# Another order for the end of a linear attention and for the routing behind it, in a two-layer vision tower

## The chip, the cores and the metric

The kernel runs as one program on one core of one Trainium2 chip. The metric is the device time of one execution in microseconds (us); where several runs are given, their median. All arithmetic is in 32-bit floating point.

A core has a matrix engine (TensorE, PE in the profile, with its weight loads as PEld), a vector engine (VectorE, DVE), an engine for activation functions (ScalarE, ACT), a general one (GpSimd, POOL), and SyncE (SP), which only issues transfers here. Each engine works through its own queue of instructions in order; an instruction that waits holds up all behind it on that engine, and nothing on the others unless they need its result.

## The reference

128 images go through a tokenizer, then two layers; each layer adds an attention and a feed-forward part to its input. What the change touches is the second layer: a linear attention over 8 heads, and the routing of 8192 tokens to 8 experts.

```python
# second layer, attention: q, k, v per head, x is normalised
q = softmax(q, axis=-1)
k = softmax(k, axis=-2)
q = q * sqrt(d)
attn_weights = einsum('bhnd,bhmd->bhnm', q, k).sum(0)       # not returned
context = einsum('bhnd,bhne->bhde', k, v)
out = einsum('bhnd,bhde->hbne', q, context)
# second layer, mixture of experts: T = 8192 tokens, E = 8, capacity C = 1280
logits = x @ gate_w + gate_b                                # x is normalised
probs = softmax(logits, axis=-1)
idx = argmax(probs, axis=-1)
prb = take_along_axis(probs, idx[:, None], axis=1)[:, 0]
one_hot = jax.nn.one_hot(idx, E)
pos = (cumsum(one_hot, axis=0) * one_hot).sum(-1) - 1       # place in the expert's buffer
kept = pos < C
hmid = relu(buf @ w1 + b1); ybuf = hmid @ w2 + b2           # per expert
y_tok = ybuf[idx, min(pos, C - 1)] * (prb * kept)[:, None]
return h + y_tok
```

## The kernel before

The program has stages one behind the other: tokenizer, an attention with relu, an attention of experts, then `linear_attention` (L1388), `route` (L1934) and `experts` (L2049). The data of the layer, h, is 128 images x 64 tokens x 256 features.

**The linear attention** takes the heads in four groups of two (`heads[0]` to `heads[3]`, class `Heads`). For each group a loop runs over 16 steps i. In a step TensorE projects queries and keys (`queries_keys`), `prepare` normalises and transposes token groups for later steps, then come the pieces of work that a table (`at(n, i, ...)`, in loop n at step i, in the order in which they were entered) puts there, and at last VectorE takes the projection out of PSUM (`queries_keys_kept`, L1478). The order of instructions on each engine is that of the program text (`manual_schedule`). The softmax, scores, mixing and sums of a group are put into the loop of the next one. For the last group, `heads[3]`, half of this is in the table and the rest in a function of its own, `last()` (L1740), which runs once behind the loops.

For one group the pieces are, with the engine that does most of each:

- `largest_of`, `maximum_of`, `spread_of`: the largest query over all (VectorE; TensorE for `pm`, L1533, and `pb`, L1542), `q_less_of` subtracts it (VectorE), `q_exp_of` (ScalarE);
- `k_max` (VectorE, L1580), `k_less` (GpSimd, L1584), `k_exp_of` (ScalarE), `k_sum` (VectorE, L1591), `k_over_sum` (GpSimd, one half of the last group VectorE, L1597);
- `values` (TensorE L1488, ScalarE copies), `values_transposed` (TensorE L1501, ScalarE L1504);
- `scores` (128 matmuls, L1606), `scores_kept` and `scores_sums` (`am`, `rq`, VectorE), then four times `mixed` (TensorE, L1628) and `added` (VectorE adds the mix to h, L1636);
- `written`: SyncE stores the group's 64 features of h to `hx` and to `out`, 2 MB each (L1640);
- `moments`: one `bn_stats` for each token (VectorE, L1644, written to `sth`), which the routing's normalisation needs;
- `transposed`: h transposed (TensorE L1650, ScalarE copies L1654), `gates`: its product with the gate's weights into a PSUM tile `pg` (L1663), `gates_added`: VectorE sums this over the four groups in `lgs` (L1673 and L1675).

Before, group 0 has its 64 moments in the loop, group 1 has 16 in the loop at step 8 and 48 in `last()`, groups 2 and 3 have all in `last()`. `routing.statistics` (L1903) then makes mean and variance of each token out of the moments, and ends with the inverse root (`inverse_root`, L1921, 14 small VectorE instructions).

**The routing** transposes the summed gates (`pl`, L1960), normalises them (`dev`, L1961, `pb`), finds each token's expert (`oh`), its place by a scan (`cs`, L1980) and two matmuls over partitions (`pp`), and the experts of the 39 blocks of 256 places (`past`, `be`, `bexp`, L2000 to L2004). Then it builds a table that says which token stands at each place: eight parts of 8 token columns each, with one-hot rows `lh` (L2029) and `hv` (L2032) by VectorE in rings of two buffers, `hv` times the token's number by ScalarE (64 activations in all, L2037), and 64 matmuls into `pi` (L2039). The table itself is `rin` and `rout` (L2042, L2046). Here no order is written out: the framework's planner orders each engine's instructions.

**The experts**, 39 blocks, load their weights (SyncE, L2097 to L2101) by the block's expert in `bexp`, and gather their tokens with indirect transfers by `rin` (GpSimd, L2110). The first three blocks' loads are issued ahead of the loop.

`c.busy` issues matmuls whose result nobody reads.

Of the kernel before, what the change touches and what calls it, by code (L numbers as in the profile page):

```python
# [12 lines left out]
F32 = mybir.dt.float32  # L13
# [7 lines left out]
P = 128  # L21
B = 128
# [1365 lines left out]
def linear_attention(c, front, hd, hx, out, k):  # L1388
# [8 lines left out]
    with (  # L1397
# [51 lines left out]
        class Heads:  # L1449


            def __init__(self, n, groups):
                self.n, self.groups = n, groups

            def begin(self):
                self.qk = hp.tile([P, 2, 32, P], F32, tag="qk", name="qk", bufs=2)
# [201 lines left out]

            def gates(self, x):

                self.pg = pso.tile([P, 4, B], F32, tag="po", name="pg")
                for s in range(4):
                    nc.tensor.matmul(  # L1663
                        self.pg[s * 32 : s * 32 + 32].rearrange("p j b -> p (j b)"),
                        wgs[:, self.n, :],
                        self.hT[s].rearrange("p j b -> p (j b)"),
                        start=True,
                        stop=True,
                    )

            def gates_added(self, x):
                if self.n == 0:
                    nc.vector.tensor_copy(lgs[:, x], self.pg)  # L1673
                else:
                    nc.vector.tensor_add(lgs[:, x], lgs[:, x], self.pg)  # L1675
# [9 lines left out]
        for n, x in enumerate(heads[:3]):  # L1685
# [30 lines left out]

            for k in range(8):
                at(m + 1, 1 + k, x.transposed, k)
            for k in range(4 if n == 0 else 1):
                at(m + 1, 8 + k, x.moments, 16 * k, 16)  # L1720
            for k in range(2):
                at(m + 1, 4 + 4 * k, x.gates, k)
                at(m + 1, 5 + 4 * k, x.gates_added, k)
# [15 lines left out]

        def last():  # L1740

            x, y, z = heads[3], heads[2], heads[1]
            x.values(0)
            x.largest_of(1)
            x.values(1)
            x.values(2)
            x.maximum_of(1)
            x.k_max(1)
            x.k_less(1, 0)
            x.k_less(1, 1)  # L1750
            x.values(3)
            x.spread_of(1)
            x.q_less_of(1, 0)
            x.values(4)
            x.q_exp_of(1, 0)
            x.q_less_of(1, 1)
            x.values(5)
            x.k_exp_of(1, 0)
            x.q_exp_of(1, 1)
            x.values(6)  # L1760
            x.k_exp_of(1, 1)
            x.values(7)
            x.k_sum(1)
            x.k_over_sum(1, 1)
            x.k_over_sum(1, 0)
            z.moments(16, 32)
            for i in range(2):
                x.values_transposed(i)
            x.scores()
            x.scores_kept()  # L1770
            x.values_transposed(2)
            x.scores_sums()
            x.values_transposed(3)
# [10 lines left out]
            for i in range(4):  # L1784
                y.transposed(i)
            y.gates(0)
            x.moments(0, 64)
            for i in range(4, 8):
                y.transposed(i)
            y.gates_added(0)  # L1790
            y.gates(1)
            y.moments(48, 16)
            for i in range(4):
                x.transposed(i)
            y.gates_added(1)
            routing.statistics(front.group(0), front.group(1))
            x.gates(0)
            x.gates_added(0)
            for i in range(4, 8):
                x.transposed(i)  # L1800
            x.gates(1)
            x.gates_added(1)

        def prepare(g, i):

# [46 lines left out]
class Routing:  # L1852
# [50 lines left out]
    def statistics(self, t, u):  # L1903

        nc, mean = self.c.nc, self.mean
        dev, sq = (t[:, 2 * i : 2 * i + 2].rearrange("p a (t n) -> p (a t) n", n=8) for i in range(2))
        var, m = (u[:, i, 0:T] for i in range(2))
        parts = self.sth.rearrange("p t n (s k) -> p t (n s) k", k=3)
        nc.vector.tensor_reduce(mean, parts[:, :, :, 1], AX.X, ALU.add)
        nc.vector.tensor_scalar_mul(mean, mean, 1.0 / 8)  # L1910
        nc.vector.tensor_sub(dev, parts[:, :, :, 1], bcast(mean, 2, 8))
        nc.vector.tensor_mul(sq, dev, dev)
        nc.vector.tensor_reduce(m, sq, AX.X, ALU.add)
        nc.vector.tensor_reduce(var, parts[:, :, :, 2], AX.X, ALU.add)
# [19 lines left out]
def route(c, k, gfd):  # L1934
# [4 lines left out]
    tc, nc = c.tc, c.nc  # L1939
    with (  # L1940
        tc.tile_pool(name="mg", bufs=1) as gp,
        tc.tile_pool(name="mn", bufs=2) as np_,
        tc.tile_pool(name="mgp", bufs=1, space=PSUM) as gpp,
    ):

        def g8(name):
# [11 lines left out]
        for x in range(2):  # L1958
            for j in range(4):
                nc.tensor.transpose(pl[:, x, j].rearrange("p s n -> p (s n)"), k.lgs[:, x, j, :], c.ident)  # L1960
        nc.vector.tensor_mul(dev, bcast(k.wsum, 1, T), bcast(mean, 2, E))  # L1961
        for x in range(2):
            ts = slice(x * 32, x * 32 + 32)
            o, i = (y[:, ts, :].rearrange("p (s j n) e -> p j s (n e)", s=4, j=4) for y in (pb, dev))
            for j in range(4):
                nc.vector.tensor_sub(o[:, j], pl[:, x, j, :, 0 : 2 * E], i[:, j])
# [14 lines left out]
        pp = gpp.tile([P, 2, E], F32, name="pp")  # L1981
        nc.tensor.matmul(pp[:, 0], k.before, cs[:, T - 1, :], start=True, stop=True)
        nc.tensor.matmul(pp[:, 1], k.ones, cs[:, T - 1, :], start=True, stop=True)
# [13 lines left out]
        nc.vector.tensor_sub(first, end, nblk)  # L1997
        nc.vector.tensor_scalar_mul(first, first, float(BLK))

        nc.vector.tensor_tensor(past, bcast(k.blk, 2, E), bcast(end, 1, NBLK), ALU.is_ge)  # L2000
        nc.vector.tensor_reduce(be[:, 0:NBLK], past, AX.X, ALU.add)
        nc.vector.tensor_scalar_min(be[:, 0:NBLK], be[:, 0:NBLK], float(E - 1))
        nc.vector.tensor_copy(be[:, NBLK : NBLK + 1], end[:, E - 1 : E])
        nc.vector.tensor_copy(c.bexp, be)  # L2004
# [15 lines left out]
        nc.vector.tensor_single_scalar(row[:, 1], row[:, 0], 7, ALU.arith_shift_right)  # L2020
        nc.vector.tensor_single_scalar(row[:, 2], row[:, 0], P - 1, ALU.bitwise_and)
        nc.vector.tensor_copy(at, row[:, 1:3])
        pi = gpp.tile([P, NTILE], F32, name="pi")
        NQ = 8
        for t0 in range(0, T, T // NQ):
# [9 lines left out]
            for i in range(T // NQ):  # L2035
                t = slice(t0 + i, t0 + i + 1)
                nc.scalar.activation(hv[:, i], hv[:, i], AF.Copy, scale=k.token[:, t])  # L2037
            for i in range(T // NQ):
                nc.tensor.matmul(pi, lh[:, i], hv[:, i], start=(t0 + i == 0), stop=(t0 + i == T - 1))  # L2039
        id1 = gp.tile([P, NTILE], F32, name="id1")  # L2040
# [286 lines left out]
```

## Time and profile before

| | us |
|---|---|
| median of 3 runs | 2665.02 |
| the runs | 2665.02, 2655.38, 2665.51 |
| the profiled execution | 2654.66 |
| its span, first to last instruction | 2652.9 |
| loop of the last head group ends (last L1478) | 2124.51 to 2125.20 |
| scores of the last group (L1606) | 2143.48 to 2148.93 |
| last sums into h (L1636) end, stores issued (L1640) | 2163.42, 2163.45 |
| `dev`, first VectorE instruction of the routing (L1961) | 2184.67 |
| first part of the table (L2029) | 2201.17 |
| first load of expert weights issued (L2097) | 2200.78 |
| table complete in PSUM, `rin` (L2042) | 2221.87 |
| first matmul of an expert (L2153) | 2231.16 |

Times inside an execution count from its first instruction. The stages named in the table fill about 110 of the 2653 us; behind them the experts run to the end. In a line of the timeline there stand the start and the length in us, the engine, the line of the program, the instruction with its output and inputs and how many of them were merged, and in brackets how long the engine was idle before it and what ended that.

### The profile page before, as it was taken

The numbers are of one execution on the slowest core, as the hardware profiler recorded it, in microseconds if no ns is written. First come the engines' busy times: TensorE is split into PE (matmuls) and PEld (weight loads), VectorE is DVE, ScalarE is ACT, GpSimd is POOL, SyncE is SP. The second block draws the span as 40 slices with busy tenths as digits, with TensorE's granted clock in tenths as the row PEclk, the third lists the DMA queues.
The fourth block names the chain that finished last, engine by engine and source line by source line (L and its number), as shares of the span: only waits on it lengthen the run. The fifth ranks groups of instructions, "written<-read, shape, count | busy, mean of one in ns | idle before, by whom it ended". The sixth has DMA issues, their size and how long they took to land. (4 is left out here: it accounts for less than half of the span.)

```text
span 2652.9 us, 81755 instructions
## 1 busy us (share of the span) xinstructions
PE 2526.2 (95%) x35633; PEld 1730.8 (65%) x35633; DVE 2012.2 (76%) x3000; ACT 1623.1 (61%) x3421; POOL 1625.8 (61%) x1428
## 2 busy tenths in 40 slices
PE   8989999999999999899999999999999877999997
PEld 4554444444444444688888888888566556888886
DVE  5759999999999999887878777878467786444443
ACT  2218889899898888666666666666344533233232
POOL 3319989899899999566565666653233313544544
PEclk9999999999999999999999999999999998999998
DMA  3100000000000000000000000000334444555554
GB/s 112 33 13 1 2 2 2 1 2 2 2 2 1 2 13 2 3 28 23 14 23 14 13 24 13 14 23 23 75 73 111 96 128 152 191 185 202 188 189 134
DMA packets 138046, 141.19 MB, mean 53 GB/s; under 512 B 108001, under 2 KB 121859, under 8 KB 129870
## 3 DMA queue, kind: packets, MB, share of 16 engines
q1 hardware_dynamic: 128684, 119.48, 15.3%
q0 software_dynamic: 7648, 14.77, 1.8%
q8 instruction: 281, 4.60, 0.7%
q10 hardware_dynamic: 1344, 1.61, 0.2%
q14 instruction: 89, 0.73, 0.1%
HBM read 104.00 MB, written 32.54 MB: 51 GB/s over the span
## 5 line engine op out<-in xcount | busy, mean ns | idle before, releaser
L540 POOL TENSOR_TENSOR m<-q,k 128x1024 f32<-128x1024 f32 x384 | 719.6, 1907 | 55.9 <-PE sc L342 46.8
L532 DVE TENSOR_TENSOR m<-pc,k 128x2048 f32<-128x2048 f32 (+1 forms) x320 | 646.3, 2055 | 0.5 <-ACT q L472 0.5
L342 PE MATMUL sc<-m,wide 128*32 128x512 f32 x4096 | 520.0, 597 | 8.9 <-ACT m L541 6.6
L541 ACT ACTIVATE m<-m 128x1024 f32<-128x1024 f32 x384 | 402.5, 1049 | 20.4 <-POOL m L540 20.4
L342 PEld LDWEIGHTS sc<-m,wide 128*32 128x32 f32 x4096 | 134.7, 109 | 269.2 <-issue 157.4
L550 ACT ACTIVATE m<-k,q 128x64 f32<-128x64 f32 x1024 | 270.8, 339 | 0.9 <-DVE k L419 0.9
L1070 DVE TENSOR_REDUCE mx<-sc 128x16 f32<-128x1024 f32 x128 | 156.0, 1219 | 133.6 <-PE sc L1058 133.6
L1085 POOL TENSOR_TENSOR e<-e,mx 128x1024 f32<-128x1024 f32 x127 | 241.6, 1903 | 9.9
L1017 ACT COPY kr<-pqk 128x512 f32<-128x512 f32 x254 | 137.9, 604 | 139.3 <-PE pqk L1011 139.3
L2153 PE MATMUL ph<-xt,w1s 128*128 128x256 f32 x896 | 200.5, 382 | 2.2 <-DVE xt L2144 1.5
L2169 PE MATMUL po<-w2s,hT 128*128 128x256 f32 x896 | 198.0, 379 | 0.0
L1084 POOL TENSOR_TENSOR mx<-mx,gate 128x16 f32<-128x16 f32 x127 | 27.4, 216 | 278.3 <-ACT z L1115 162.7
L2153 PEld LDWEIGHTS ph<-xt,w1s 128*128 128x128 f32 x896 | 171.0, 191 | 27.3 <-DVE xt L2144 2.1
L2169 PEld LDWEIGHTS po<-w2s,hT 128*128 128x128 f32 x896 | 168.1, 190 | 21.7
L1097 ACT COPY pT<-pt 128x512 f32<-128x512 f32 x256 | 138.8, 600 | 51.0 <-PE pt L1094 50.8
L1071 DVE TENSOR_TENSOR e<-sc,mx 128x1024 f32<-128x1024 f32 x128 | 156.7, 1224 | 4.4
L2187 POOL DMA_INDIRECT out<-y,rout x56 | 56.6, 1011 | 168.2 <-ACT hT L2157 129.2
L1077 DVE TENSOR_REDUCE mx<-e 128x16 f32<-128x1024 f32 x128 | 152.5, 1191 | 4.0 <-ACT e L1074 3.6
L2157 ACT ACTIVATE hT<-ph,w1s 128x256 f32<-128x256 f32 x224 | 93.0, 470 | 98.6 <-PE ph L2153 95.1
L1094 PE MATMUL pt<-ident,e 128*128 128x128 f32 x1024 | 141.3, 280 | 11.2 <-DVE vr L1047 7.0
L2174 ACT ACTIVATE y<-y,gf 128x256 f32<-128x256 f32 x56 | 28.0, 507 | 195.0 <-issue 110.3
L1074 ACT ACTIVATE e<-e 128x1024 f32<-128x1024 f32 x128 | 139.6, 1091 | 1.2 <-DVE e L1071 1.2
(337 smaller groups left out, 5009.4 us busy)
## 6 DMA issues: line engine op xcount, KB each, us to landing
w1s<-in_we SPq DMA_DIRECT2D x30, 1028.0 KB
w2s<-in_we SPq DMA_DIRECT2D x30, 1024.0 KB
h<-hd SPq DMA_DIRECT2D x4, 2048.0 KB
hx<-h SPq DMA_DIRECT2D x4, 2048.0 KB
out<-h SPq DMA_DIRECT2D x4, 2048.0 KB
xt<-in_x SPq DMA_DIRECT2D x15, 512.0 KB
hd<-h SPq DMA_DIRECT2D x15, 512.0 KB
x<-hd SPq DMA_DIRECT2D x12, 512.0 KB
```

Source lines behind the costliest of these rows:

```text
L342: nc.tensor.matmul(dst[j : j + 32], wide[:, hf, s : s + 32], part, start=start, stop=stop)
L532: nc.vector.tensor_tensor(m, bcast(self.pq[:, hf, i : i + n], 3, T), k, ALU.max)
L540: nc.gpsimd.tensor_tensor(m, bcast(self.q[:, hf, s : s + 2], 3, T), k, ALU.subtract)
L541: nc.scalar.activation(m, m, AF.Relu)
L550: nc.scalar.activation(self.parts[i, hf][:, q], self.blk.k[:, hf, i], AF.Relu, bias=self.q[:, hf, i - NB // 2, q : q + 1], scale=-1.0,)
L1070: nc.vector.tensor_reduce(mx, sc, AX.X, ALU.max)
L1071: nc.vector.tensor_sub(e, sc, bcast(mx, 2, T))
L1077: nc.vector.tensor_reduce(self.sm[x], self.e[x], AX.X, ALU.add)
L1085: eng.tensor_mul(e, e, bcast(sm, 2, T))
L1094: nc.tensor.transpose(pt[:, cq, :], e[:, i : i + 2, :].rearrange("p e s -> p (e s)"), c.ident)
L2153: nc.tensor.matmul(ph[:, j], self.w1[:, w0 : w0 + P], self.xt[:, fc], start=(fc == 0), stop=(fc == 1))
L2169: nc.tensor.matmul(po, self.hT[:, f, r * P : r * P + P], self.w2[:, f, :], start=(f == 0), stop=(f == 7))
```

## The change

Four places are edited.

In the table of the loops, group 1's moments go to steps 9 to 12 of group 3's loop, 16 in each (before: 16 at step 8, the rest in `last()`).

In `last()` the keys' chain is taken first: `k_max` and `k_less` ahead of the queries' maximum, the keys' exponentials between the copies of the values. The scores come before any transpose of values. Group 2's moments stand behind the keys' division, behind the scores' sums and behind the first mix. The gates of group 2 stay in PSUM, those of group 3 are accumulated on top (`start` only for groups below 3, `stop` for all but group 2), and one VectorE sum takes both.

In the routing the order is written out (`manual_schedule`); the inverse root moves out of `statistics` to behind `dev`; the blocks' experts move into a function that is called behind the first table part; `idle` is 8 matmuls on `lgs` in place of 6 on `past`.

In the table the rings have three buffers, and the last of the eight parts has `hv` times the token numbers as one VectorE product in place of 8 activations.

```diff
+                if self.n == 3:
+                    self.pg = heads[2].pgs[x]
+                else:
+                    self.pg = pso.tile([P, 4, B], F32, tag="po", name="pg")
+                    self.pgs[x] = self.pg
...
-                        start=True,
-                        stop=True,
+                        start=(self.n < 3),
+                        stop=(self.n != 2),
...
-                    nc.vector.tensor_add(lgs[:, x], lgs[:, x], self.pg)
+                    nc.vector.tensor_add(lgs[:, x], lgs[:, x], self.pgs[x] if self.n < 3 else heads[2].pgs[x])
...
-            for k in range(4 if n == 0 else 1):
-                at(m + 1, 8 + k, x.moments, 16 * k, 16)
+            for k in range(4):
+                at(m + 1, (8 if n == 0 else 9) + k, x.moments, 16 * k, 16)
...
-            x, y, z = heads[3], heads[2], heads[1]
+            x, y = heads[3], heads[2]
+            x.k_max(1)
             x.values(0)
+            x.k_less(1, 0)
+            x.k_less(1, 1)
             x.largest_of(1)
             x.values(1)
+            x.k_exp_of(1, 0)
             x.values(2)
+            x.k_exp_of(1, 1)
+            x.values(3)
             x.maximum_of(1)
...
+            x.k_sum(1)
             x.spread_of(1)
             x.values(4)
+            x.k_over_sum(1, 1)
+            for i in range(2):
+                x.q_less_of(1, i)
+                x.q_exp_of(1, i)
             x.values(5)
+            x.k_over_sum(1, 0)
             x.values(6)
             x.values(7)
-            z.moments(16, 32)
+            y.moments(0, 32)
+            x.scores()
+            x.scores_kept()
             for i in range(2):
                 x.values_transposed(i)
-            x.scores()
-            x.scores_kept()
...
             x.scores_sums()
+            for i in range(2, 4):
+                x.values_transposed(i)
-            z.moments(48, 16)
+            y.moments(32, 16)
             for i in range(4):
                 x.mixed(i)
...
-                if i < 3:
-                    y.moments(16 * i, 16)
+                if i == 0:
+                    y.moments(48, 16)
                 x.added(i)
             x.written()
+            for k in range(2):
+                for i in range(4):
+                    y.transposed(4 * k + i)
+                y.gates(k)
             x.moments(0, 64)
...
             routing.statistics(front.group(0), front.group(1))
+            for k in range(2):
+                for i in range(4):
+                    x.transposed(4 * k + i)
+                x.gates(k)
+                x.gates_added(k)
...
-        inverse_root(self.c, var, self.rs, m)
+        self.var, self.m = var, m
+
+    def root(self):
+        inverse_root(self.c, self.var, self.rs, self.m)
...
-        tc.tile_pool(name="mn", bufs=2) as np_,
+        tc.tile_pool(name="mn", bufs=3) as np_,
         tc.tile_pool(name="mgp", bufs=1, space=PSUM) as gpp,
+        tc.manual_schedule(),
...
         nc.vector.tensor_mul(dev, bcast(k.wsum, 1, T), bcast(mean, 2, E))
+        k.root()
...
-        idle = gpp.tile([P, NBLK, E], F32, name="idle")
-        c.busy(idle, past, 6)
+        idle = gpp.tile([P, 2 * B], F32, name="idle")
+        c.busy(idle, k.lgs[:, 0, 0:2], 8)
...
+        def experts_of_blocks():
+            nc.vector.tensor_tensor(past, bcast(k.blk, 2, E), bcast(end, 1, NBLK), ALU.is_ge)
+            nc.vector.tensor_reduce(be[:, 0:NBLK], past, AX.X, ALU.add)
+            nc.vector.tensor_scalar_min(be[:, 0:NBLK], be[:, 0:NBLK], float(E - 1))
+            nc.vector.tensor_copy(be[:, NBLK : NBLK + 1], end[:, E - 1 : E])
+            nc.vector.tensor_copy(c.bexp, be)
...
+            if t0 == T - T // NQ:
+                nc.vector.tensor_mul(hv, hv, bcast(k.token[:, ts], 2, NTILE))
+            else:
+                for i in range(T // NQ):
+                    t = slice(t0 + i, t0 + i + 1)
+                    nc.scalar.activation(hv[:, i], hv[:, i], AF.Copy, scale=k.token[:, t])
+            if t0 == 0:
+                experts_of_blocks()
```

More of the change, by code (lines that the diff above doesn't have):

```diff
@@ L1452, in __init__ @@
             def __init__(self, n, groups):
-                self.n, self.groups = n, groups
+                self.n, self.groups, self.pgs = n, groups, {}
             def begin(self):
@@ L1659, in gates @@
             def gates(self, x):
-                self.pg = pso.tile([P, 4, B], F32, tag="po", name="pg")
+                if self.n == 3:
[3 more added lines that the diff above has]
+                    self.pgs[x] = self.pg
                 for s in range(4):
@@ L1740, in last @@
         def last():
-            x, y, z = heads[3], heads[2], heads[1]
+            x, y = heads[3], heads[2]
+            x.k_max(1)
             x.values(0)
+            x.k_less(1, 0)
+            x.k_less(1, 1)
             x.largest_of(1)
             x.values(1)
+            x.k_exp_of(1, 0)
             x.values(2)
+            x.k_exp_of(1, 1)
+            x.values(3)
             x.maximum_of(1)
[L1748 to L1751, printed above, removed]
+            x.k_sum(1)
             x.spread_of(1)
-            x.q_less_of(1, 0)
             x.values(4)
-            x.q_exp_of(1, 0)
-            x.q_less_of(1, 1)
+            x.k_over_sum(1, 1)
+            for i in range(2):
+                x.q_less_of(1, i)
+                x.q_exp_of(1, i)
             x.values(5)
-            x.k_exp_of(1, 0)
-            x.q_exp_of(1, 1)
+            x.k_over_sum(1, 0)
             x.values(6)
-            x.k_exp_of(1, 1)
             x.values(7)
-            x.k_sum(1)
-            x.k_over_sum(1, 1)
-            x.k_over_sum(1, 0)
-            z.moments(16, 32)
+            y.moments(0, 32)
+            x.scores()
+            x.scores_kept()
             for i in range(2):
                 x.values_transposed(i)
-            x.scores()
-            x.scores_kept()
-            x.values_transposed(2)
             x.scores_sums()
-            x.values_transposed(3)
-            z.moments(48, 16)
+            for i in range(2, 4):
+                x.values_transposed(i)
+            y.moments(32, 16)
             for i in range(4):
@@ L1779, in last @@
                         x.values_transposed(j)
-                if i < 3:
-                    y.moments(16 * i, 16)
+                if i == 0:
+                    y.moments(48, 16)
                 x.added(i)
             x.written()
-            for i in range(4):
-                y.transposed(i)
-            y.gates(0)
+            for k in range(2):
+                for i in range(4):
+                    y.transposed(4 * k + i)
+                y.gates(k)
             x.moments(0, 64)
[L1788 to L1795, printed above, removed]
-            routing.statistics(front.group(0), front.group(1))
[L1797 to L1802, printed above, removed]
+            routing.statistics(front.group(0), front.group(1))
+            for k in range(2):
[3 more added lines that the diff above has]
+                x.gates_added(k)
         def prepare(g, i):
@@ L1998, in route @@
         nc.vector.tensor_scalar_mul(first, first, float(BLK))
[L2000 to L2004, printed above, removed]
-        idle = gpp.tile([P, NBLK, E], F32, name="idle")
-        c.busy(idle, past, 6)
+        idle = gpp.tile([P, 2 * B], F32, name="idle")
+        c.busy(idle, k.lgs[:, 0, 0:2], 8)
         nc.vector.tensor_add(cs, cs, bcast(pp[:, 0], 1, T))
@@ L2034, in route @@
             )
-            for i in range(T // NQ):
-                t = slice(t0 + i, t0 + i + 1)
-                nc.scalar.activation(hv[:, i], hv[:, i], AF.Copy, scale=k.token[:, t])
+            if t0 == T - T // NQ:
[6 more added lines that the diff above has]
+                experts_of_blocks()
             for i in range(T // NQ):
```

## The prediction

> **What bounds the kernel now.** The page comes first: TensorE is busy 95% of the span and VectorE 76%, but these are means over stages, and the change touches only the last part of linear attention and the routing, about 2091 to 2222 us. So I read the timeline of each engine there, looking for idle time and for what ended it, then the stores of SyncE, then the windows for the granted clock and the DMA rate. VectorE first (start, length, instruction, idle before it and releaser):
>
> ```profile
> 2091.10 2.11 DVE L1644 BATCH_NORM_STATS2 sth<-h 128x6 f32<-128x64 f32 x16
> 2093.21 0.69 DVE L1478 TENSOR_TENSOR qk<-pq,bs 128x512 f32<-128x512 f32 x1
> 2095.43 0.69 DVE L1675 TENSOR_TENSOR lgs<-lgs,pg 128x512 f32<-128x512 f32 x1 [1.52 <-PE pg L1663]
> 2102.95 0.22 DVE L1612 COPY am<-pa 128x64 f32<-128x64 f32 x1 [0.94 <-PE pa L1606]
> 2105.90 0.56 DVE L1618 RECIPROCAL rq<-pr 128x64 f32<-128x64 f32 x1 [2.13 <-PE pr L1616]
> 2109.04 0.28 DVE L1536 TENSOR_REDUCE mc<-pm 64x1 f32<-64x128 f32 x1 [2.33 <-PE pm L1533]
> ...
> 2124.51 0.69 DVE L1478 TENSOR_TENSOR qk<-pq,bs 128x512 f32<-128x512 f32 x1 [0.35 <-PE pq L1474]
> 2125.24 1.65 DVE L1524 TENSOR_TENSOR m<-qk 128x512 f32<-128x512 f32 x1
> ```
>
> The 16 moments at loop step 8 cost nothing, as the next projection was late anyway. Steps 9 to 12 hold waits of 1.5, 0.9, 2.1 and 2.3 us, each ended by TensorE. The rest of the stage:
>
> ```profile
> 2139.49 2.29 DVE L1591 TENSOR_REDUCE ks<-qk 128x32 f32<-128x2048 f32 x1 [4.68 <-ACT qk L1554]
> ...
> 2163.45 8.21 DVE L1644 BATCH_NORM_STATS2 sth<-h 128x6 f32<-128x64 f32 x64
> ...
> 2184.67 0.69 DVE L1961 TENSOR_TENSOR dev<-wsum,mean 128x512 f32<-128x512 f32 x1 [0.54 <-DMA out<-h]
> 2185.66 1.14 DVE L1966 TENSOR_TENSOR pb<-pl,dev 128x64 f32<-128x64 f32 x8 [0.29 <-PE pl L1960]
> ...
> 2195.54 0.20 DVE L1994 TENSOR_TENSOR full<-pp,step 128x40 f32<-128x40 f32 x1 [1.13 <-PE pp L1983]
> ...
> 2201.17 1.23 DVE L2029 TENSOR_TENSOR lh<-lo,at 128x1024 f32<-128x1024 f32 x1
> ...
> 2205.80 1.23 DVE L2029 TENSOR_TENSOR lh<-lo,at 128x1024 f32<-128x1024 f32 x1 [0.83 <-PE pi L2039]
> ```
>
> From 2163.45 VectorE has no idle of weight up to 2184.67: it is the bound. The reader should mark that line: `dev` waited for the store of h. Windows show when that store ends (VectorE busy 1.90 and 1.17 us; the last three columns are clock, DMA share, GB/s):
>
> ```profile
> 2182.00:2184.00 2.00, 0.32 (x2) 0.35 (x3) 1.90 (x6) 0.00 (x0) 0.00 (x0) 0.50 0.79 211
> 2184.00:2186.00 2.00, 1.62 (x8) 1.22 (x6) 1.17 (x5) 0.00 (x0) 0.00 (x0) 0.50 0.01 1
> ```
>
> Both stores (2 MB to hx, 2 MB to out) are issued at 2163.45 and land 21.2 us later. I call A the end of the last `added`, 2163.42. Last, TensorE and GpSimd:
>
> ```profile
> 2143.48 5.45 PE L1606 MATMUL pa<-qk 128*64 128x64 f32 x126 [2.14 <-DVE qk L1597]
> ```
> ```profile
> 2142.31 2.87 POOL L1597 TENSOR_TENSOR qk<-qk,ks 128x1024 f32<-128x1024 f32 x1 [5.91 <-DVE ks L1592]
> ```
>
> **What the Trainium skill says.** "SBUF — State Buffer", Who interferes with whom: a VectorE instruction with two SBUF inputs and a GpSimd one that reads SBUF exclude each other for a whole instruction. The trace agrees: L1524, 0.68 us at 2096.03, took 1.65 beside a GpSimd multiplication; L1597 on GpSimd, 1.88 alone, took 2.87. "TensorE: Matmul & The Clock Gate", What's actually happening: about 3.4 us without work halves the clock, as much work restores it. The trace agrees: the scores took 5.45 us at 2143.48 (clock 0.50 from 2144 to 2146) and 3.95 at 2098.95 (1.00). "DMA: Bandwidth & Descriptors", Queues, rings and completion order: an engine of DMA takes turns between queues, so a gather behind weights gets a share only; no run shows that here.
>
> **The change, part by part** (all times those of this execution).
>
> *Moments of head group 1 in the loop.* 48 more bn_stats, 3 x 2.11 = 6.33 us, go to steps 9 to 12, and step 8 loses its 16, where VectorE will wait for the projection until 2093.18. They stand first in each step. Walking VectorE's queue with the durations above: step 9, moments 2093.81 to 2095.92 take the 1.52 wait, +0.5. Step 10, +2.1, less the 0.94 wait: `am` +1.7. Step 11, the moments stand ahead of the reciprocal, whose input is there at 2105.9: `am` is done at 2108.25 instead of 2106.72, and `mixed(0)` on TensorE, with `pm` behind it, starts 1.5 later; the 2.33 wait just moves. Step 12, another 2.11 ahead of `added(0)`, and `mixed(1)` waits for the PSUM that it frees: +3.6. From 2113.59 to the loop's end VectorE has 0.6 us of idle, so all of it carries. Bounds: 0 if the waits took all, 4.2 if only step 9's did. I take **+3.6**.
>
> *Keys first.* k_max (2.27) runs at once, then GpSimd's k_less (2 x 1.88) beside `largest_of` (3.1, two SBUF inputs). Taking turns they end 2.27 + 3.1 + 3.76 = 9.1 after 2125.2, at 2134.3; `pm` stands behind values(3), done at 2131.4, so TensorE waits 2.9, then to 2135.3 for `dg`. k_sum follows at 2135.1 (4.4 earlier). Four values of 1.78 end at 2142.7, and q_less, q_exp and k_over_sum (at 2141.3) are hidden there. The scores start at 2142.7 without a gap before them: 3.95, end 2146.65, against 2148.93: **-2.3**. If VectorE keeps its turn throughout, the end is 2145.55, -3.4; if the 2.9 wait halves the clock for one window, -0.6.
>
> *Mixing.* Two transposes of values now stand behind the scores, each of 4 activations (1.09) with two PSUM buffers: mixed(0) starts 3.4 after the scores instead of 1.66, but later waits for VectorE go, since only 16 moments are left in the way. mixed(3) ends at +13.35, the last sum at +14.65, against +14.49: **+0.2**. A moves by 3.6 - 2.3 + 0.2 = +1.5.
>
> *After A.* Gone from VectorE: 16 moments 2.12 and two PSUM sums 2 x 0.68; the root (3.36) moves behind `dev`. Left are 8.2 + 4.7 of statistics. TensorE begins group 2's transposes only at A - 1.3 and needs 4 x 4.06 us, so the last gates come at A + 15 and the sum at A + 15.6. But `dev` cannot start before the stores land, A + 21.2, as before: the 5.6 us saved become a wait, and the root, hidden until now in front of the wait, stands behind it. `pb` starts at A + 21.25 + 0.73 + 3.3 = A + 25.3, against A + 22.24: **+3.05**. If `dev` did not have to wait, it would be A + 19.7: -2.5.
>
> *Routing by hand.* gf's sum and reciprocal (0.61 + 0.46) go into the 1.13 wait for `pp`: -0.75. The blocks' experts (L2000 to L2004, start to start 1.06) go behind the first table part; dependent small instructions no longer interleave, +0.6 of it back. **-1.15**, bounds -0.6 and -1.7. TensorE's idle work (16 passes) ends before the first `pi`.
>
> *Table.* With three buffers the 0.83, 0.75 and 0.74 waits go; seven ACT parts of 2.06 remain and the eighth is a VectorE product (128x624, 0.80 like L2032). From lh: 1.98, 2.06, a stall of 1.2 for the experts' 1.4 us, six parts 12.4, last TensorE part 2.1, end at 20.0 against 20.66: **-0.5**, bounds 0 and -1.5.
>
> *Expert weights.* SyncE's loads follow bexp, now 3.3 us behind the first lh instead of 1.7 ahead: 5 us later. They keep the DMA busy 18 us at 364 GB/s; before they ended at 2220.3, 2.7 ahead of the first gather, so now about 2.5 us of them lie beside it. First weights stay covered. Bounds 0 and 2 (half rate for both gathers), I take **+0.6**.
>
> Sum: 3.6 - 2.3 + 0.2 + 3.05 - 1.15 - 0.5 + 0.6 = **+3.5 us**. Against this execution (2654.66, its span 2652.9 and 1.76 around it) that is 2658.2. The median shown is 10.4 above it, and the three runs spread over 10.1 us, so one execution doesn't settle the level: I add to the median, 2665.0 + 3.5 = 2668.5. About 0.5% (13.3 us) is what a measurement of this kernel can tell from no change.
>
> **Rivals.**
> 1. *The waits do take the work* (chance 0.25). For it: VectorE's waits of 1.5, 0.9, 2.1, 2.3, 2.2, 4.7 and 1.5 us between 2093 and 2150, 15 us in all. Loop +1.5 instead of 3.6, lock harmless (-3.4), the store's wait partly shorter (+1), the rest as above: about -1.5; with `dev` free to start, -4.5 to -5: 2660. Against it: the releaser in the 2184.67 line.
> 2. *TensorE goes cold, slower* (0.12). Place: new TensorE waits of 2.4 us at mixed(0), 2.3 at mixed(1), 2.9 at `pm`, and the gap before `pi`. Each that falls on an idle window halves the clock for 3.4 us of work, 1.7 us; all four with the gathers at their bound: 3.5 + 6.8 + 1.4 = +11.7, 2676.7. It decides from about 3.4 us of idle; single waits stay below.
> 3. *Nothing is gained or lost* (0.08): the planner's order was already as good and the wait for the stores absorbs A's shift; 0, 2665.
>
> **How the numbers follow.** The forecast has 0.55, with 2664 to 2671 as its own range on the median's level; at the level of the profiled execution it lies 10 lower. The range over all reaches 2652 (the forecast and part of rival 1 at the lower level) and 2675. Faster by over 0.5% needs rival 1 together with the low level: half its chance, and 0.03 for what I have not seen, 0.15. Slower: somewhat under half of rival 2 and 0.04, 0.09. Within: 0.76.
>
> **What would show it.** Right: `dev` with an idle of some 5 us released by DMA out<-h, the root behind it; step 12's q_less about 3.6 later relative to step 8; L1524's group stretched beside GpSimd; the scores near 3.95 us; the first w1s issue after, not before, the first lh. Wrong: `dev` without a wait, the loop's steps unshifted, half clock at values(4) or `pi`, a wait for the first gather much over 3.3 us.

## The result, and the profile after

The kernel with the change takes 2677.6 us (median of 6 runs, 2675.5 to 2682.8), the kernel before 2664.8 in the same series (6 runs, 2655.4 to 2665.9). The ratio on record is 1.0061 with a 95% interval from 1.0048 to 1.0074; the medians of these twelve runs alone give 1.0048. So the kernel became slower; the middle of the interval lies above the 0.5% that the prediction took as the least that can be told apart, its lower end just below. The forecast was 2668.5, with a range to 2675.

The profiled execution took 2675.45 us (its span 2673.6, mean granted TensorE clock 0.981; before: 2652.9 and 0.989). Cut at the same instructions, the two profiles compare as follows. A is again the end of the last `added`.

| stretch | before, us | after, us | difference | forecast |
|---|---|---|---|---|
| loop: projection kept at step 8 to the last one kept (L1478) | 31.30 | 37.93 | +6.63 | +3.6 |
| to the end of the scores (L1606) | 24.42 | 24.38 | -0.04 | -2.3 |
| to A | 14.49 | 14.51 | +0.02 | +0.2 |
| A to `pb` | 22.24 | 25.26 | +3.02 | +3.05 |
| `pb` to the first `lh` | 15.51 | 14.37 | -1.14 | -1.15 |
| first `lh` to `rin` (the table) | 20.70 | 29.86 | +9.16 | -0.5 |
| `rin` to the first expert's matmul | 9.29 | 9.99 | +0.70 | +0.6 |

Together +18.35 us, against +3.5. Four of the seven terms are met within 0.2 us; the table, the loop and the keys are not. These are differences between one execution of each kernel.

VectorE's timeline of the changed kernel, with the lines that answer to those shown of before:

```profile
2107.97 2.11 DVE L1644 BATCH_NORM_STATS2 sth<-h 128x6 f32<-128x64 f32 x16
2110.00 0.54 DVE L1618 RECIPROCAL rq<-pr 128x64 f32<-128x64 f32 x1
2110.58 0.73 DVE L1619 TENSOR_TENSOR am<-am,rq 128x64 f32<-128x64 f32 x1
...
2137.68 4.58 DVE L1526 TENSOR_TENSOR m<-m,qk 128x512 f32<-128x512 f32 x2
...
2158.46 0.23 DVE L1612 COPY am<-pa 128x64 f32<-128x64 f32 x1 [4.10 <-PE pa L1606]
...
2194.22 0.69 DVE L1961 TENSOR_TENSOR dev<-wsum,mean 128x512 f32<-128x512 f32 x1 [4.99 <-DMA out<-h]
...
2198.18 1.13 DVE L1967 TENSOR_TENSOR pb<-pl,dev 128x64 f32<-128x64 f32 x8
...
2228.76 1.22 DVE L2033 TENSOR_TENSOR lh<-lo,at 128x1024 f32<-128x1024 f32 x1 [1.47 <-PE pi L2048]
...
2242.41 0.24 DVE L2051 TENSOR_SCALAR rin<-pi 128x78 int32<-128x78 f32 x1 [7.45 <-PE pi L2048]
```

Read the brackets. `dev` waits 4.99 us for the store of h where it waited 0.54. In the table VectorE waited some 0.8 us for `pi` in every other part before, and 2.74 at the end; now, once the three buffers are full, it waits 1.47 us in each part, and 7.45 at the end. TensorE has become the bound there. TensorE's timeline of the changed kernel:

```profile
2111.36 2.95 PE L1628 MATMUL po<-am,vT 64*128 64x64 f32 x32 [2.62 <-DVE am L1619]
...
2114.46 3.62 PE L1474 MATMUL pq<-w,xT 128*128 128x512 f32 x4
...
2143.36 0.42 PE L1533 MATMUL pm<-ident,m 128*64 128x128 f32 x1 [2.46 <-DVE m L1528]
...
2145.05 9.48 PE L1488 MATMUL pv<-wvs,xT 128*128 128x256 f32 x32
...
2206.95 5.79 PE L50 MATMUL idle<-lgs,ident 128*128 128x256 f32 x16
2214.94 2.20 PE L2048 MATMUL pi<-hv,lh 128*128 128x78 f32 x16 [2.20 <-ACT hv L2044]
2218.19 24.18 PE L2048 MATMUL pi<-hv,lh 128*128 128x78 f32 x112 [1.05 <-ACT hv L2044]
```

And of the kernel before:

```profile
2106.77 2.00 PE L1628 MATMUL po<-am,vT 64*128 64x64 f32 x32 [0.91 <-DVE am L1619]
...
2197.80 5.20 PE L50 MATMUL idle<-past,ident 128*128 128x312 f32 x12 [2.29 <-DVE past L2000]
2203.56 4.20 PE L2039 MATMUL pi<-hv,lh 128*128 128x78 f32 x32 [0.56 <-ACT hv L2037]
```

Most of the groups above have a shorter twin: `mixed(0)` took 2.00 before, a projection `pq` 1.88, 32 matmuls of values 7.17. For `pi` the changed kernel shows both rates: 16 in 2.20 us, then 112 in 24.18, which is 0.14 and 0.22 us each. The windows show what goes with it (PE, PEld, DVE, ACT, POOL busy, then the granted clock, the DMA share, GB/s):

```profile
2212.00:2215.00 3.00, 0.80 (x5) 0.37 (x3) 2.90 (x7) 0.47 (x2) 0.00 (x0) 1.00 0.00 0
2215.00:2218.00 3.00, 2.14 (x16) 1.99 (x16) 2.93 (x7) 1.86 (x8) 0.00 (x0) 1.00 0.00 0
2218.00:2221.00 3.00, 2.81 (x13) 2.81 (x14) 3.00 (x4) 3.00 (x13) 0.00 (x0) 0.50 0.95 326
2221.00:2230.00 9.00, 9.00 (x44) 9.00 (x44) 5.58 (x7) 7.12 (x28) 0.00 (x0) 0.50 0.90 362
```

TensorE idles for most of the first window and part of the second, the clock falls to one half in the third, and in the fourth TensorE is busy for all 9.00 us and does not get it back. It comes back only behind the table. Below, "cold" means at half clock and "warm" at full clock. So the first theory after the result was: the table is slow because a wait at its start, 2.20 us ahead of its first matmul or 1.05 behind the sixteenth, loses the clock. The rival was that `pi` itself or its operands had become slower, by the three buffers, by VectorE's product, or by the weight loads beside it (326 to 362 GB/s), which come later than before.

### The profile page after: what moved, and what is told of

It is laid out like the page before. It is cut to its first block, busy times and chain, and to the rows that moved or that the text cites. A ratio compares the mean times of both kernels' runs of the same rounds, so it can differ in the third digit from the quotient of the medians.

```text
span 2673.6 us, 81748 instructions
## 1 busy us (share of the span) xinstructions
PE 2544.1 (95%) x35637; PEld 1746.6 (65%) x35637; DVE 2014.7 (75%) x2999; ACT 1621.5 (61%) x3413; POOL 1625.6 (61%) x1428
```

## The experiments

Unless it is said otherwise an edit is made to the changed kernel. The comparisons with the kernel before are each with its runs on the same chip.

**e1: more idle repeats ahead of the table.**

```diff
-        c.busy(idle, k.lgs[:, 0, 0:2], 8)
+        c.busy(idle, k.lgs[:, 0, 0:2], 14)
```

> The changed kernel with 14 idle matmuls of 256 columns in place of 8 ahead of the table. Cold theory (the 2.2 us without work ahead of the first pi, after the shorter idle work, lets the TensorE clock fall to half, and pi's matmuls cannot bring it back): the clock is 1.00 at the first pi; if this gap alone decides, it stays 1.00 and the table (first lh to rin) takes 20 to 21 us instead of 29.9, the total 8 to 10 us less than the changed kernel's 2677; if the second gap (1.05 us, the blocks' experts between parts 0 and 1) suffices by itself, the clock still falls after part 0 and the table stays near 29. Rival (the table is slow for VectorE's product, the third buffer or the later weight loads): no change, 29 to 30 us, whatever the clock.

2671.8 us, ratio 1.0034 [1.0021, 1.0047]. TensorE's timeline of e1:

```profile
2210.47 8.57 PE L50 MATMUL idle<-lgs,ident 128*128 128x256 f32 x28
2218.88 1.91 PE L2048 MATMUL pi<-hv,lh 128*128 128x78 f32 x16
2221.71 14.00 PE L2048 MATMUL pi<-hv,lh 128*128 128x78 f32 x112 [0.93 <-ACT hv L2044]
...
2246.61 10.14 PE L2162 MATMUL ph<-xt,w1s 128*128 128x256 f32 x32 [0.78 <-DVE xt L2153]
```

The same 112 matmuls, from the same rings, beside the same weight loads, take 14.00 instead of 24.18 us; the table takes 19.68, which is 1.0 below the kernel before, where 0.5 was forecast. The rival falls. The total is some 6 us below the changed kernel where 8 to 10 were expected, for about 3 us come back behind the table: the first expert's matmuls took 7.17 in the changed kernel and take 10.14 here. There the idle matmuls behind the table, slow by the half clock (8.29 us), covered the wait for the gather by chance. Here they take 5.39, TensorE waits 3.44 for the gathered tokens, and the clock falls at the expert instead. e1 changes two things at once, the wait ahead of the table and the amount of warming work; the kernel before tells them apart, as its 5.20 us of idle matmuls are less than the changed kernel's 5.79 and were enough with 0.56 us behind them.

**e2: the blocks' experts ahead of the table**, which closes the 1.05 us wait inside it but widens the one ahead of it.

```diff
+        experts_of_blocks()
         pi = gpp.tile([P, NTILE], F32, name="pi")
...
-            if t0 == 0:
-                experts_of_blocks()
```

> The changed kernel with the blocks' experts worked out ahead of the table instead of between its parts 0 and 1 (8 idle matmuls as changed). Cold theory: the gap between parts 0 and 1 goes, but the gap between idle work and first pi grows from 2.2 to about 3.6 us, so the clock falls about as before: table 27 to 30 us, total as the changed kernel's. If the gap between the parts is what decides, the table takes 20 to 21 us. Rival (later weight loads slow the table): loads 3.3 us earlier relative to the first lh, the table some us shorter with the clock still at 0.50.

2677.2 us, ratio 1.0058 [1.0042, 1.0075], the table 30.02. TensorE's timeline of e2 has `pi` in one piece, cold from its start, behind a wait of 3.19:

```profile
2218.71 27.60 PE L2047 MATMUL pi<-hv,lh 128*128 128x78 f32 x128 [3.19 <-ACT hv L2045]
```

So curing the inner wait alone does not help, while e1 kept one of 0.93 us and stayed warm. But here the outer wait has grown as well; that it is enough by itself, e7 will show.

**e5: the kernel before, without its idle matmuls.** No edit of the change is in it.

```diff
-        c.busy(idle, past, 6)
```

> The kernel before without its 6 idle matmuls ahead of the table; nothing else changed. Cold theory: TensorE comes to the first pi at clock 0.50 and stays there, each part takes 3.4 us instead of 2.1, so the table takes 27 to 29 us instead of 20.7 and the total rises by 6 to 9 us, with none of the change's edits. Rival (the edits of the table are what costs): table 20 to 22 us, total within 1 us of before.

2667.3 us, ratio 1.0021 [1.0011, 1.0031], 5.2 us above the kernel before in the same series (2662.1), where 6 to 9 were expected. TensorE's timeline of e5:

```profile
2205.93 27.59 PE L2038 MATMUL pi<-hv,lh 128*128 128x78 f32 x128 [8.06 <-ACT hv L2036]
```

27.59 us for 128 matmuls, as in e2, and the table takes 30.02 instead of 20.70. The cost can be made in the old kernel by taking away the warming work alone. With it, the old kernel had only 0.56 us between the idle matmuls and `pi`, because they waited for `past`, which is computed just ahead of the table; the new ones wait for nothing but `pp` and are done 2.20 us early.

**e6: the kernel before once more**, for the scatter between its own executions.

> The kernel before, unchanged, for a second profile of it: its runs lie between 2655 and 2666. Cold theory: the clock's windows run freely, so in some executions a part of this stretch (table or scores) falls on half clock without any change; an execution near 2665 shows a stage that takes 5 to 10 us longer at clock 0.50. Rival: the 10 us lie in stages far from it, or are spread evenly.

2659.4 us, ratio 0.9993 [0.9986, 1.0]. Its profiled execution took 2667.98 us, 13 more than the first one of the same kernel, with an equal table (20.69) and equal routing. Step 8 came at 2104.19 instead of 2093.21, and the loop took 33.89 instead of 31.30. So 11.0 of the 13 us lie ahead of step 8, where the clock record of this execution has three cold stretches (at 1300.7, 1881.0 and 2024.4 us, 13.7 us in all) and that of the first one has none. The stage longer by 5 to 10 us that was expected behind step 8 is not there. A single span of this kernel can lie 13 us beside another, and only stretches behind a common instruction may be compared; even the loop carries 2.6 us of this.

**e3: group 1's moments back behind the loop.** Its 48 late moments stand in `last()`, 32 of them ahead of the kept scores.

```diff
-            for k in range(4):
-                at(m + 1, (8 if n == 0 else 9) + k, x.moments, 16 * k, 16)
+            for k in range(4 if n == 0 else 1):
+                at(m + 1, 8 + k, x.moments, 16 * k, 16)
...
             y.moments(0, 32)
+            z.moments(16, 32)
...
+                if i == 1:
+                    z.moments(48, 16)
```

> The changed kernel with group 1's moments back at loop step 8 (16 of them) and the other 48 in the last function: 32 behind group 2's first 32, 16 ahead of the second sum. Cold theory (the moments made TensorE wait at mixed(0), which halved its clock for the steps behind): step 8's projection to the last one takes 31.3 us as before instead of 37.9, with at most one cold window (2.6 us more); the scores' end stays 24.4 behind, the sums' end goes from 14.5 to some 15.5 behind the scores: 5 to 6 us less than the changed kernel. Rival (the loop grew by VectorE's queue alone, 3.6 us): 34.3 us or more remains gone from it, and a gain of 3 us at most is seen there.

2673.7 us, ratio 1.0045 [1.003, 1.0059]; some 4 us less than the changed kernel where 5 to 6 were expected. The loop takes 32.29, the wait at `mixed(0)` is 0.91 as before. TensorE's timeline of e3:

```profile
2116.20 2.00 PE L1628 MATMUL po<-am,vT 64*128 64x64 f32 x32 [0.91 <-DVE am L1619]
...
2145.64 8.76 PE L1488 MATMUL pv<-wvs,xT 128*128 128x256 f32 x32
```

The moments are 5.6 of the loop's 6.6 us. Where the 48 stood in this execution they cost nothing: the stretches to the end of the scores and to A are 23.33 and 14.50, no longer than the 24.38 and 14.51 without them. The values ran in part cold here too, 8.76 instead of 7.17.

**e4: the root ahead of `dev`.**

```diff
+        k.root()
         nc.vector.tensor_mul(dev, bcast(k.wsum, 1, T), bcast(mean, 2, E))
-        k.root()
```

> The changed kernel with the inverse root ahead of dev instead of behind it. If dev is held by the store of h (lands 21.3 us after the last sum) the root is hidden in the wait: dev still 21.3 behind the last sum, pb 22.2 behind it instead of 25.3, 3.0 us less in all, the table cold as in the changed kernel. Rival (dev is held by VectorE's own queue): dev moves to 24.7 and nothing is gained.

2673.0 us, ratio 1.004 [1.0025, 1.0056]. A to `pb` is 22.13 instead of 25.26: the root cost its whole length because it stood behind the wait for the store. By chance this execution also shows the keys' stage at full clock, with the same waits. TensorE's timeline of e4:

```profile
2147.06 0.30 PE L1533 MATMUL pm<-ident,m 128*64 128x128 f32 x1 [2.46 <-DVE m L1528]
2148.01 0.43 PE L1542 MATMUL pb<-dg,ones 64*128 64x64 f32 x2 [0.66 <-DVE dg L1537]
2148.38 7.17 PE L1488 MATMUL pv<-wvs,xT 128*128 128x256 f32 x32
```

The stage takes 21.70 here, 2.7 below the kernel before. The 2.3 us forecast for keys first are there when the clock stays; in the changed kernel's profile the clock takes them away (9.48 instead of 7.17 for the values).

**e7: queries first again.** The order is `largest_of`, `k_max`, `k_less`, `maximum_of`, `spread_of`; the exponentials and sums move with it, and the first two transposes of values stand ahead of the scores.

```diff
+            x.largest_of(1)
+            x.values(0)
             x.k_max(1)
-            x.values(0)
+            x.values(1)
             x.k_less(1, 0)
             x.k_less(1, 1)
-            x.largest_of(1)
-            x.values(1)
+            x.values(2)
+            x.maximum_of(1)
+            x.spread_of(1)
...
             for i in range(2):
+                x.values_transposed(i)
...
             x.scores()
             x.scores_kept()
-            for i in range(2):
-                x.values_transposed(i)
```

> The changed kernel with the queries' maximum ahead of the keys in the last function, the keys' exponentials still ahead of the queries', and the first two transposes of values ahead of the scores again. Lock theory (GpSimd's k_less and VectorE's largest_of, both with two SBUF inputs, take turns, so pm is late, TensorE waits some 3 us and goes cold): largest_of takes 3.1 to 4.1 us instead of 6.3, values(4) to values(7) 7.1 us instead of 9.5, last projection to the scores' end 21.5 to 22.5 us instead of 24.4. Rival (the keys' chain through GpSimd and ScalarE is the limit whatever the order): 24 us remain.

It missed: 2680.5 us, ratio 1.0076 [1.0061, 1.0091], and the stage took 27.76. VectorE's timeline of e7:

```profile
2145.58 1.80 DVE L1537 TENSOR_SCALAR dg<-ident,mc 64x64 f32<-64x64 f32 x1
...
2157.93 2.29 DVE L1591 TENSOR_REDUCE ks<-qk 128x32 f32<-128x2048 f32 x1 [7.41 <-ACT qk L1554]
```

`largest_of` no longer stands beside GpSimd's subtraction, but now `dg`, 0.25 us elsewhere, lies beside `k_less` on GpSimd and takes 1.80. TensorE then waited 3.92 for the spreading and ran five blocks of values in part cold (11.72 us; four take 7.17 warm), and `k_sum` waited 7.41 for exponentials that stand behind the copies of the values on ScalarE. The mixing took 12.68 instead of 14.51; but two transposes moved ahead of the scores, so that their work now counts in the stretch before.

e7 also settles which wait the table loses its clock by. TensorE's timeline of e7:

```profile
2212.58 6.69 PE L50 MATMUL idle<-lgs,ident 128*128 128x256 f32 x16
2220.58 2.64 PE L2049 MATMUL pi<-hv,lh 128*128 128x78 f32 x16 [1.31 <-ACT hv L2045]
2223.82 24.18 PE L2049 MATMUL pi<-hv,lh 128*128 128x78 f32 x112 [0.60 <-ACT hv L2045]
```

And two of its windows of 1 us, with the granted clock third from the end:

```profile
2221.00:2222.00 1.00, 1.00 (x11) 1.00 (x10) 0.93 (x5) 1.00 (x6) 0.00 (x0) 1.00 0.00 0
2222.00:2223.00 1.00, 1.00 (x7) 1.00 (x6) 1.00 (x2) 0.28 (x2) 0.00 (x0) 0.53 0.00 0
```

The clock falls at 2222.1, while the first 16 `pi` still run and ahead of the inner wait. So the outer wait suffices, and 1.31 us of it did. In e4 the clock fell among these 16 as well, behind an outer wait of 2.74. Over all profiles: with 1.31 to 8.06 us between the idle matmuls and `pi` the table ran cold in six of six (the changed kernel, e2, e3, e4, e5, e7), with 0.56 us or less in none of seven.

**e8: the mended parts together, and other memory for the waiting tile.** e3's moments, e1's 14 repeats, the root back in `statistics`, and `pb`, `dev` and `m` in the memory of the gate's pool instead of that which h's store is still reading. Of the edit only the memory is shown.

```diff
+        self.pb, self.dev = (gp.tile([P, T, E], F32, name=n) for n in ("pb", "dev"))
+        self.m = gp.tile([P, T], F32, name="m")
...
-        pb, oh, cs, dev, sq = g8("pb"), g8("oh"), g8("cs"), g8("dev"), g8("sq")
-        m, gf, pos = (g1(n) for n in ("m", "gf", "pos"))
+        oh, cs, sq = (g8(n) for n in ("oh", "cs", "sq"))
+        gf, pos = (g1(n) for n in ("gf", "pos"))
+        pb, dev, m = k.pb, k.dev, k.m
```

> The changed kernel with 14 idle matmuls, the moments as in e3, the root back in the statistics, and pb, dev and m in memory that no store of h holds. Cold theory and store theory together: loop 31.3 us instead of 37.9, sums 1 us later, pb 18.5 to 19.5 us behind the last sum instead of 25.3, table 19.7 instead of 29.9: 20 to 22 us less than the changed kernel, 6 to 9 us less than the kernel before (ratio to it 0.9965 to 0.998). If the memory is not what held dev, pb comes at 22.2 and the kernel is 3 us less fast.

2665.9 us, ratio 1.0018 [1.0011, 1.0025], where 0.9965 to 0.998 were expected. The wait for the store is gone (`dev` at A + 10.16, `pb` at A + 18.92), the loop takes 31.29 and the keys' stage 21.70. But from the scores to A it took 23.51 instead of 14.5. TensorE's timeline of e8:

```profile
2159.71 0.43 PE L1616 MATMUL pr<-am,share 128*128 128x64 f32 x2 [1.71 <-DVE am L1612]
...
2161.05 3.68 PE L1628 MATMUL po<-am,vT 64*128 64x64 f32 x32
```

The scores end earlier than in e3, so the 64 moments ahead of `am` are now late (VectorE is busy with them from 2151.34 to 2159.54), TensorE waits 1.71 us between small pieces, and the mixing runs cold to its end: 3.68 for what takes 2.00.

**e9: as e8, with those moments spread**: 8 of group 1's ahead of the kept scores, 16 each ahead of the second and third `added`, 8 ahead of the last group's own.

```diff
-            z.moments(16, 32)
+            z.moments(16, 8)
...
-                if i == 1:
-                    z.moments(48, 16)
+                if i in (1, 2):
+                    z.moments(16 * i + 8, 16)
...
+            z.moments(56, 8)
             x.moments(0, 64)
```

> The kernel of e8 with group 1's 48 late moments spread: 8 instead of 32 ahead of the kept scores, 16 each ahead of the second and the third addition, 8 ahead of the last group's own. If those 32 made TensorE wait at the sums of the scores and so lost the clock through the mixing, that wait is under 0.8 us, the 32 matmuls of a mixing stretch take about 2.0 instead of 3.7 us, and from the end of the scores to the last addition it is 14 to 15 us instead of 23.5; the loop stays at 31.3, the scores at 21.7, the table at 19.7, and the kernel comes out 7 to 10 us below e8, some 3 to 6 us below the kernel before. If the clock falls there for another reason, the mixing stays above 20 us and the time near e8's.

2660.2 us, ratio 0.999 [0.9983, 0.9997]: 0.1% or 2 us below the kernel before, where 3 to 6 us were expected. No wait is left ahead of `pr`, and to A it is 14.93. TensorE's timeline of e9:

```profile
2143.91 8.80 PE L1488 MATMUL pv<-wvs,xT 128*128 128x256 f32 x32
...
2157.45 0.33 PE L1616 MATMUL pr<-am,share 128*128 128x64 f32 x2
...
2160.09 2.00 PE L1628 MATMUL po<-am,vT 64*128 64x64 f32 x32
```

The medians of e8 and e9 lie 5.7 us apart, and the stretches of the two profiles 5.4: the mixing gains 8.6, but the loop (32.30) and the keys' stage (23.33, the values at 8.80) each met a cold spell in this execution that e8's had not, and `pb` came 1.0 later behind A.

**e10: as e9, with the blocks' experts ahead of the table and 18 idle repeats.**

> As e9, with the blocks' experts computed ahead of the table (1.3 us of VectorE on the path) and 18 instead of 14 idle repeats to cover that. If e8's gather waited longer because the experts' weights were asked for later, the stretch from the table's last result to the first matmul of the experts is about 9.5 instead of 11.2 us, at 1.3 us more ahead of the table: 0.3 to 0.6 us faster than e9, within what a measurement tells. If the gather's wait depends on the table alone, it stays near 11 and the kernel is 1 us slower than e9. The 1.05 us wait inside the table goes; the table stays at 18.6 to 19.7 us.

2659.3 us, ratio 0.9991 [0.998, 1.0001]. The wait inside the table went (18.43), the path to it grew (15.71), and the stretch to the first expert shrank from 10.78 to 9.30. The first weights are asked for 17.2 instead of 15.2 us ahead of `rin`, and VectorE takes up the first gathered tokens 4.39 instead of 6.43 us behind it, so earlier weights do shorten the gather's wait. In all, e9 and e10 cannot be told apart.

**e11: as e9, with a block of values in each of the two waits of the keys' stage.**

```diff
             x.values(3)
+            x.values(4)
             x.maximum_of(1)
+            x.values(5)
             x.k_sum(1)
             x.spread_of(1)
-            x.values(4)
...
-            x.values(5)
```

> The kernel of e9 with the fifth block of values ahead of the transposition of the maxima and the sixth between it and their spreading, so that TensorE has 1.8 us of work in each of the two waits (2.46 and 0.66 us) that the keys-first order and the lock of the subtraction leave. If those waits are what lets the clock fall there (values 8.80 instead of 7.17 us in e9), the wait for the maxima shrinks to under 1 us, that for their spreading goes, the values run at full clock, and from the last kept projection to the end of the scores it is 20 to 21 us instead of 23.3: 2 to 3 us below e9. If VectorE's and ScalarE's queue behind the subtraction set the end instead, the stage stays within 0.7 us of 23.3.

TensorE's timeline of e11:

```profile
2132.21 8.80 PE L1488 MATMUL pv<-wvs,xT 128*128 128x256 f32 x40
2141.73 0.30 PE L1533 MATMUL pm<-ident,m 128*64 128x128 f32 x1 [0.73 <-DVE m L1528]
2141.87 1.89 PE L1488 MATMUL pv<-wvs,xT 128*128 128x256 f32 x8
```

The stage takes 20.21 and no block of values is cold, as expected. The whole is 2656.7 us, ratio 0.9992 [0.9982, 1.0002]: the 3 us of the stage are not seen in the total. In its profile the first expert's matmuls took 9.73 us behind a wait of 3.43 for the gather (8.69 and 3.36 in e9), so part is given back there; the rest lies within the scatter.

## Why the prediction was wrong

The step that failed is **Table**, "-0.5, bounds 0 and -1.5"; it came out at +9.16. Its working followed VectorE's and ScalarE's queues and took TensorE's part at the warm rate, "last TensorE part 2.1". It had no term for TensorE's clock. The routing step even noted that the idle work "ends before the first `pi`", and gave that no price. Rival 2 did name the gap before `pi`, but priced each loss at 1.7 us, one window, and let it decide only "from about 3.4 us of idle". A line that the prediction itself shows spoke against this threshold: the scores at 2143.48 were at half clock behind a wait of 2.14. The runs showed threshold and price wrong: 2.20 us ahead of the table were enough in the changed kernel and 1.31 in e7, and the table's own matmuls, though TensorE was busy throughout, never brought the clock back, so that the loss lasted for the whole table. e1, e2, e5 and e7 show that from four sides: outer gap closed, inner one closed, gap made in the old kernel, clock lost ahead of the inner gap.

**Loop**, +3.6, the mechanism right and a term too small: +6.63. The walk through VectorE's queue holds; the moments stand ahead of the reciprocal and `mixed(0)` is late. But within the 2.62 us wait the clock fell, and from 2112 to 2126 TensorE ran at half, `mixed(0)`, a projection and `mixed(1)` at 2.95, 3.62 and 4.02 us. e3 takes the moments out and gets 5.6 of the 6.6 back. How the 6.6 split can be estimated from VectorE's timelines, counted from step 8: `am` is done 1.70 us later than before (forecast 1.5), and the 2.11 us of moments ahead of `added(0)` make 3.8, which is the forecast's 3.6; the other 2.8 come with the half clock. The size varies between executions: the changed loop took 36.46 to 37.93 us in five profiles, the old one 31.29 to 33.89 in three.

**Keys first**, -2.3 with -0.6 for "one window" lost: -0.04. That the two engines shut each other out is there as forecast. GpSimd's timeline of the changed kernel:

```profile
2137.12 4.59 POOL L1584 TENSOR_TENSOR qk<-qk,ks 128x1024 f32<-128x1024 f32 x2 [1.08 <-DVE ks L1580]
```

4.59 instead of 3.76, and the two L1526 of VectorE's `largest_of` 4.58 instead of 1.42: the Trainium skill's page "SBUF — State Buffer", Who interferes with whom, is agreed with once more. The wait for `pm` came near to what was worked out, 2.46 against 2.9. What was mis-sized is the clock, put at one window or 0.6 us: where it stayed, in e4 and e8, the stage was 2.7 shorter than before; in the changed kernel, e1, e2, e3, e9 and e10 it fell, and the values cost 1.6 to 2.9 more.

**After A**, +3.05, measured +3.02, and `pb` at A + 25.26 where A + 25.3 was written: right, for the reason given. e4 moves the root and gets 3.1 back. The statement "if `dev` did not have to wait, it would be A + 19.7" was tried in e8 and came out at 18.92 (there with the root ahead).

**Routing by hand** (-1.14 against -1.15) and **mixing** (+0.02 against +0.2) were right by their sums. **Expert weights**, +0.70 against +0.6, was right by luck. VectorE takes up the first gathered tokens 4.38 us behind `rin` in the changed kernel and 4.46 before, so the later loads cost the gather nothing: the slow table gave them time to end first. TensorE was late because its idle matmuls, cold for most of their length, ran until 2251.19. With a table at full rate the tokens came 6.51 (e1) and 6.43 us (e9) behind `rin`, and the first expert +1.5 to +1.9 (e1, e8, e9, e11), within the bounds given.

Rival 2 was the right side and nearly the right time, 2676.7, but by luck, as its prices were wrong: four losses of 1.7 us where one cost ten and two cost about 3 and 2. Half clock at `values(4)` or `pi`, which the prediction named as a sign of being wrong, came at both.

By the ratios to the kernel before, curing one part at a time gains 0.27% (the table, e1), 0.16% (the loop, e3) and 0.21% (the root, e4), together 0.64% against the change's 0.61%; each ratio is known to about 0.15%.

The stretches add up to +18.35 and the medians differ by 12.7. The two profiled executions lie 20.8 us apart: 18.35 in the stretches, 2.9 ahead of step 8, some -0.4 behind the last stretch. The profiled execution of before (2654.66) is faster than all six runs and 10.2 below their median, that of the changed kernel only 2.1 below its own, which makes the 12.7. e6 shows one way in which the kernel before takes longer, cold stretches far ahead of the change; for the other executions there is no trace, and this stays open.

## What to carry to other kernels

Where warming work stands ahead of a stream of small matmuls, its end counts once it has brought the clock up, not its amount (5.20 us with 0.56 behind them sufficed, 6.69 with 1.31 behind them did not): tie it to the last thing that the stream itself waits for, and after each reorder read on TensorE's timeline what gap is left between the two. Price a gap by the work up to the next dense stretch, not by one window: a stream that keeps the clock when warm may be unable to restore it. And before filling an engine's waits with other work, ask whether TensorE's next piece stands behind that work; e9's division of the same 48 moments left the stretch to A within 0.5 us of the kernel before, where the change's placing cost 5.6 us in the loop.

## What the runs showed that was not expected

- A busy TensorE can stay at half clock. `pi` (128x78, one weight load each) was busy for 9.00 of 9 us at 0.50, in all 24 to 27.6 us in six kernels; the same stream kept the clock at 1.00 for 14.00 us in e1. The 64-column mixing in e8 behaved alike. The scores, 64 columns wide too, did restore it in the kernel before, from 2143.41 to 2146.82. The Trainium skill, "TensorE: Matmul & The Clock Gate", What's actually happening, has about 3.4 us of sustained work restore the clock; for these two streams the measurement says otherwise. What it is in them that doesn't count as busy was not tried.
- The same wait goes either way. Behind 2.46 us ahead of `pm` the clock fell in six kernels and stayed in e4 and e8. The clock records show a grid: in every trace the clock changes only after multiples of 3.41 us, the ends of the trace aside, and where the grid lies differs between executions. In the stretch of the grid that held most of this wait TensorE was busy for 1.39 us in the changed kernel, for less in e1, e2, e3, e9 and e10, and the clock fell; it was busy for 1.46 in e4 and 1.60 in e8, and the clock stayed. Busy time alone is not the measure, though: where the changed kernel lost the clock at the table, the stretch held 2.20 us of `pi`.
- Curing one cold stretch moved another: the idle matmuls slowed by the lost clock had hidden the gather's wait in the changed kernel, and with the cure the first expert ran cold (10.14 instead of 7.17 us).
